# A gated cross-attention and mixture-of-experts kernel: setup in half chunks, in-place M for the first batch, transfers split, the last placing moved

## The chip, the cores and the metric

The kernel runs on one core of one Trainium2 chip. The core has five engines that run side by side, each with its own in-order instruction queue: TensorE (PE, matrix products and transposes, which write into PSUM), VectorE (DVE), ScalarE (ACT), GpSimd (POOL) and SyncE (SP). SP and POOL also issue the transfers (DMA) between memories. The metric is the device time of one execution in microseconds (us). Before the change the median of three runs is 1732.46 us (1730.8 to 1734.78).

## The reference

Four batches of 2048 tokens of width 512 pass through two blocks with residual connections. The first is cross-attention with 16 heads of width 64 to 77 context rows per batch; the second sends each token to the two best of ten experts, of which eight are true and two are null.

```python
def _L0_xattn_ref(x, context, ln_gamma, ln_beta, w_q, w_kv, w_out, b_out, gate):
...
    xn = _layernorm(x, ln_gamma, ln_beta)
    q = (xn @ w_q).reshape(B, SQ, NUM_HEADS, DIM_HEAD)
    kv = context @ w_kv
    k, v = jnp.split(kv, 2, axis=-1)
...
    scores = jnp.einsum('bqhd,bkhd->bhqk', q * SCALE, k)
    attn = jax.nn.softmax(scores, axis=-1)
    out = jnp.einsum('bhqk,bkhd->bqhd', attn, v).reshape(B, SQ, INNER)
    out = out @ w_out + b_out
    return out * jnp.tanh(gate[0])

def _L0_ffn_ref(inputs, gate_w, gate_b, expert_w, expert_b):
...
    gate_logits = x @ gate_w.T + gate_b
    gate_probs = jax.nn.softmax(gate_logits, axis=-1)
    weights, selected = jax.lax.top_k(gate_probs, TOP_K)
...
    expert_out = jnp.einsum('td,edh->teh', x, expert_w) + expert_b[None, :, :]
    out = jnp.einsum('te,teh->th', combine_w, expert_out)
    return out.reshape(inputs.shape[:-1] + (out.shape[-1],))
x = x + jnp.tanh(g_xattn[0]) * _L0_xattn_ref(_layernorm(x, axis=-1), ctx_1024, L0_xattn_ln_gamma, L0_xattn_ln_beta, L0_xattn_w_q, L0_xattn_w_kv, L0_xattn_w_out, L0_xattn_b_out, L0_xattn_gate)
x = x + jnp.tanh(g_ffn[0]) * _L0_ffn_ref(_layernorm(x, axis=-1), L0_ffn_gate_w, L0_ffn_gate_b, L0_ffn_expert_w, L0_ffn_expert_b)
```

## The kernel before

Everything is float32. The tokens are 64 tiles of 128. Because the context is short, the kernel folds the weights into it once per batch: M (`m_sb`, 512 x 1232) is w_q times the keys of all heads, so that the scores of a tile are one product with its normalized, transposed rows; VW (`vw`, 1232 x 512 and a row of bias) is the values times w_out, so that the attention output is one product of the transposed weights `aT` with it.

**Setup.** The context is transposed (`setup_context`), keys and values come out of w_kv (`setup_kv`), w_q is transposed (`setup_q`). `setup_m(c)` makes M for one chunk of 128 input columns, c = 0 to 3. For each of the 16 heads one product (64 rows, 308 columns: 77 context rows of four batches) lands in one of the three `mm` PSUM tiles, and `put` copies it into a stage, ScalarE (L535) and VectorE (L537) in turn. The stage is a borrowed SBUF buffer: that of `vw` for even chunks, of `gwb` for odd ones. Then SP moves batch 0's part of the stage into `m_sb` (L556) and those of the other three batches to DRAM (`m_all`, L558). After chunk 1, `step(-2)` prepares the first token tiles: a transpose, statistics, a normalization, a square root, a load.

`setup_vw(j)` makes VW for one pair of heads, j = 0 to 7: five products into `mm` tiles (`pv`, L565), copied into one of eight row buffers, and stored from there to DRAM (`vw_all`, L576), the even batches by SP and the odd ones by POOL. Scores and softmax of tiles 0 and 1 stand between the pairs, at j = 2 and j = 5; `attn_squares` follows at j = 4 and j = 7. `load_vw(0, ...)` brings batch 0's VW back from DRAM, blocks 0 to 6 after pair 6 and blocks 7 to 9 after pair 7.

**Token loop.** `step(i)` works on several tiles at once: scores of tile i + 1 (L281), the transpose of i + 2 (L261), `attend(i - 1)` (L353), gate logits of i - 2, and the rest on the other engines. `attn_squares` transposes 32 x 32 squares on VectorE (L336), and 16 moves by SP (L342) bring them to their places in `aT`. When a batch ends, `load_vw` brings the next batch's VW; it overwrites what `attend` has just read, and waits for it.

**Experts.** Normalized rows are scattered by expert into DRAM (`dispatch`, L466), from row buffers `rows`, nine of them. The last phase walks 118 slots of 128 rows: `slot_load` (SP, L834) brings a block into one of the buffers of `ring`, `slot_tr` transposes it (L863) and ScalarE copies it out (L866), `slot_pe` multiplies by the expert's weights (L889), `slot_out` adds the result up (L897, L898), and POOL gathers and scatters the sums (L847, L905). While the first slots run, `tail(q)` finishes the last token tile: its gate logits at q = 0 to 2, `choose` and `ratio` (L421, ScalarE) at q = 3, the placing (`weigh`, `place` L444, `dispatch` and the first table of blocks) at q = 5, the other tables at q = 7 and 8.

**Order.** The program runs under `manual_schedule`: each engine executes its instructions in the order in which the code issues them, and the framework adds the waits between engines.

Of the kernel before, what the change touches and what calls it, by code (L numbers as in the profile page):

```python
# [8 lines left out]
F32 = mybir.dt.float32  # L9
# [9 lines left out]
P = 128  # L19
# [5 lines left out]
def kernel(  # L25
# [88 lines left out]
    def mm_tile(name):  # L114
        return ps_m.tile([P, 512], F32, tag="mm", name=name)
# [215 lines left out]
    def attn_squares(i):  # L331


        a = attns[i % 2]
        n = -(-(COLS + 1) // 32) * 32
        nc.vector.transpose(a[:, :n], a[:, :n])  # L336
        v = a.rearrange("p (k j t) -> p k j t", j=4, t=32)
        aT = work.tile([P, NKC, P], F32, tag="aT", name=f"aT_{i}", bufs=2)
        for j in range(4):
            nk = len(range(j, n // 32, 4))  # L340
            for t in range(4):
                nc.sync.dma_start(  # L342
                    aT[j * 32 : (j + 1) * 32, :nk, t * 32 : (t + 1) * 32],
                    v[t * 32 : (t + 1) * 32, :nk, j, :],
                )
        aTs[i] = aT

    def attend(i):
        po = mm_tile(f"po{i}")
        aT = aTs.pop(i)  # L350
        for k in range(NKC):
            m = KLAST if k == NKC - 1 else P
            nc.tensor.matmul(  # L353
                po,
                aT[:m, k, :],
                vw[:m, k, :],
                start=(k == 0),
                stop=(k == NKC - 1),
            )
        pos_[i] = po  # L360

    def residual(i):
# [169 lines left out]
    def put(dst, src, dve=False):  # L532
# [3 lines left out]
        else:  # L536
            nc.vector.tensor_copy(dst, src)  # L537

    def setup_m(c):

        stage = (gwb_flat if c % 2 else vw_flat)[:, : B * COLS].rearrange("p (b n) -> p b n", b=B)
        for h in range(H):
            r = slice(h % 2 * DH, (h % 2 + 1) * DH)
            pm = mm_tile(f"pm{c}_{h}")
            nc.tensor.matmul(  # L545
                pm[:, :BK],
                wqT[r, h // 2, c * P : (c + 1) * P],
                kT[r, h // 2, :],
                start=True,
                stop=True,  # L550
            )
            put(
                stage[:, :, h * SK : (h + 1) * SK],
                pm[:, :BK].rearrange("p (b k) -> p b k", b=B),
            )
        nc.sync.dma_start(m_sb[:, c, :], stage[:, 0, :])  # L556
        for b in range(1, B):
            nc.sync.dma_start(m_all[b][:, c * COLS : (c + 1) * COLS], stage[:, b, :])  # L558

    def setup_vw(j, dve=False):  # L560

# [51 lines left out]
    def is_tile(i):  # L613
        return 0 <= i < NT

    def step(i):
# [15 lines left out]
            slot_tr(0)  # L632
            slot_tr(1)
        if is_tile(i - 1):
            attend(i - 1)
            if is_tile(i) and i % TPB == 0:
                load_vw(i // TPB)
        if is_tile(i - 2):
            choose(i - 2)
        if is_tile(i + 4):  # L640
# [27 lines left out]
            load_x(i + 5)  # L668
        if is_tile(i + 1):
            attn_squares(i + 1)  # L670
        e = i - (NT - TPB + 1)
        if 0 <= e < NE:
            nc.sync.dma_start(we[:, e], expert_w[e].rearrange("(c p) n -> p c n", p=P))
# [132 lines left out]
    ring = rows[1 : NRB - 3] + [  # L806
        attns[a][:, v * ROW : (v + 1) * ROW] for a in range(2) for v in range(2)
    ]
    ring += rows[NRB - 3 :] + [rows[0]]
    px_pool = []  # L810
    hss, toks, accs, hsTs, exps, pes, turn = {}, {}, {}, {}, {}, {}, [0, 0]

# [129 lines left out]
    def tail(q):  # L942

        i = NT - 1
        if q < 3:
            gate_logits(i, 3 * q, 3 * q + 3 if q < 2 else NG)
        elif q == 3:
            choose(i)
            ratio(i)
        elif q == 5:  # L950
            weigh(i // 2)
            place(i // 2)
            pc = count_rows(csum[0][:, 0])
            dispatch(i // 2)
            first_table(pc)
        elif q == 7:
            second_table()
        elif q == 8:
            part_table()

    with tc.manual_schedule():
# [14 lines left out]
            fill_pair(j)  # L976
        for c in range(NC):
            setup_q(c)
        for c in range(NC):
            setup_m(c)  # L980
            if c == 1:
                step(-2)
        for j in range(NPAIR):

            if j == 2 or j == 5:
                i = j // 3
                scores(i, 0)
                input_transpose(i + 1)
                scores(i, 1)
                softmax_exp(i, (0, 1))  # L990
                scores(i, 2)
                softmax_exp(i, (2,))
                ys[i + 2] = work.tile([P, D], F32, tag="y", name=f"y_{i + 2}", bufs=1)
                norm_apply(f"a{i + 2}", ys[i + 2], xs[i + 2])
                norm_stats(f"a{i + 3}", xs[i + 3])
                norm_root(f"a{i + 3}")
            if j == 4 or j == 7:
                softmax_div(j // 5)
                norm_shift(f"a{j // 5 + 3}")
                attn_squares(j // 5)  # L1000
            setup_vw(j, j in (2, 3, 5, 6))
            if j + len(vbd) < NPAIR:
                fill_pair(j + len(vbd))
            if j == 3:
                load_x(4)
                load_x(5)
                nc.sync.dma_start(vw[KLAST - 1 : KLAST, NKC - 1, :], b_out.unsqueeze(0))
            elif j == 6:
                load_vw(0, 0, 7)
        load_vw(0, 7)  # L1010
        nc.sync.dma_start(gwb, gate_w.partition_broadcast(P))
        for i in range(1, NT - 1):
            if i == SNAP + 3:
# [87 lines left out]
```

## Time and profile before

| | |
|---|---|
| median of three runs | 1732.46 us |
| the profiled execution | 1732.76 us |
| its span on the core | 1731.0 us |
| TensorE busy | 1685.1 us |
| VectorE, ScalarE, GpSimd busy | 1228.3, 934.6, 466.4 us |
| mean granted TensorE clock | 0.989 |
| first product of M, first of VW, start of the token loop | 49.68, 84.46, 171.46 us |

The profile is one execution, recorded by the hardware. "Busy" is the time in which an engine had an instruction running; for TensorE, whose products are pipelined, their ends are modelled, so that a busy TensorE can still be below its best rate. A row of the timeline begins with the start and the duration in us, then names the engine, the line of the kernel, the operation, the tile written and the tiles read, and how often; square brackets tell how long the engine had been idle and what ended it. "SPq" is SP issuing transfers. A row of waits gives the total, the number and the longest. In a row by stage, each engine has its busy time, followed by the granted TensorE clock as a share of full speed, the busy share of the transfer engines and GB/s.

### The profile page before, as it was taken

The page shows a single profiled execution, that of the slowest core. Times are in us where ns is not written, and L with a number is a line of the kernel's source. Part 1 is how long each engine was busy: PE and PEld are TensorE (multiplying, and loading weights), DVE is VectorE, ACT ScalarE, POOL GpSimd, SP SyncE. Part 2 cuts the span into 40 slices and gives each one's busy share as a digit, 9 for nine tenths or more (in the row PEclk, how much of TensorE's full clock was granted, in tenths as well). Part 3 has the DMA queues.
Part 4 walks back from the last instruction along what each step waited for, and adds up shares of the span by engine and source line. Part 5 has one row for each costly group of instructions (what it writes and reads, how often), then busy time and mean ns, then how long its engine had stood idle before and what let it go on. Part 6 is the DMA issues. An engine that isn't in the chain of part 4 may idle for free.

```text
span 1731.0 us, 22490 instructions
## 1 busy us (share of the span) xinstructions
PE 1685.1 (97%) x4938; PEld 851.0 (49%) x4938; DVE 1228.3 (71%) x3180; ACT 934.6 (54%) x3252; POOL 466.4 (27%) x617
## 2 busy tenths in 40 slices
PE   8897999999999999999999999999989999999997
PEld 6443545454445454545454545555434444444443
DVE  1443889898898989898989888989884333333333
ACT  2463777777776777677767776776421111111110
POOL 3031111121111111111112111211166556555564
PEclk9998999999999999999999999999989999999999
DMA  7477333346533435543335555554458665576752
GB/s 239 186 221 228 89 91 95 84 109 152 149 87 97 100 90 142 154 104 91 88 89 125 157 145 163 158 162 102 118 172 271 201 200 171 168 228 208 204 163 79
DMA packets 424540, 254.51 MB, mean 147 GB/s; under 512 B 349317, under 2 KB 353413, under 8 KB 424145
## 3 DMA queue, kind: packets, MB, share of 16 engines
q1 hardware_dynamic: 389873, 149.47, 35.0%
q0 software_dynamic: 34528, 103.55, 18.3%
q8 instruction: 44, 0.72, 0.2%
q14 instruction: 95, 0.78, 0.2%
HBM read 119.41 MB, written 100.52 MB: 127 GB/s over the span
## 4 chain that ended last, share of the span: by engine, by line
PE 93%; DMA 3%; DVE 2%; issue 1%; ACT 1%; SPq 0%; POOL 0%; POOLq 0%; DVEq 0%; ACTq 0%
PE po L353 31%; PE sc L281 30%; PE px L889 11%; PE pe L889 11%; PE str L863 3%; PE pkv L510 2%; PE pv L565 2%; PE xtr L261 2%; PE pm L545 1%; DMA vw<-vw_all 1%; DMA out_dram<-x 1%; DVE prod L373 0%; DMA vw<-in_ctx_dram 0%; SPq L342 0%; DMA acc<-out_dram,row 0%
## 5 line engine op out<-in xcount | busy, mean ns | idle before, releaser
L353 PE MATMUL po<-vw,aT 128*128 128x512 f32 (+1 forms) x1280 | 563.7, 595 | 10.7 <-DMA vw<-vw_all 5.5
L281 PE MATMUL sc<-m_sb,xnT 128*128 128x385 f32 (+1 forms) x1536 | 552.9, 510 | 0.0
L373 DVE CUSTOM_DVE_ANT_0 prod<-row,gwb,gbias 128x512 f32<-128x512 f32 x640 | 478.0, 747 | 17.9 <-ACT row L255 1.8
L353 PEld LDWEIGHTS po<-vw,aT 128*128 128x128 f32 (+1 forms) x1280 | 244.1, 191 | 314.3 <-issue 305.0
L281 PEld LDWEIGHTS sc<-m_sb,xnT 128*128 128x128 f32 x1536 | 284.0, 190 | 212.5 <-issue 86.3
L466 POOL DMA_INDIRECT hb<-row,dst x128 | 128.8, 1006 | 757.1 <-DVE nbh_h L250 677.8
L314 ACT ACTIVATE attn<-sc,nmx 128x77 f32<-128x77 f32 x1024 | 316.0, 347 | 28.4 <-DVE nmx L309 23.1
L866 ACT COPY m_sb<-str 128x512 f32<-128x512 f32 x118 | 68.5, 588 | 365.0 <-PE str L863 217.7
L314 ACT ACTIVATION_READ_ACCUMULATOR attn<-sc,nmx 128x1 f32 x1024 | 233.2, 228 | 0.0
L889 PE MATMUL px<-big,m_sb 128*128 (+1 forms) x472 | 214.7, 598 | 0.0
L889 PE MATMUL pe<-big,m_sb 128*128 (+1 forms) x472 | 212.3, 592 | 0.0
L897 DVE TENSOR_TENSOR yb<-px,blks 128x512 f32<-128x512 f32 x59 | 40.8, 692 | 130.1 <-PE px L889 97.4
L233 ACT ACTIVATE sdh_h<-mvh_h,eps_t 128x1 f32<-128x1 f32 x64 | 18.9, 295 | 205.9 <-DVE rsa_a L245 193.2
L889 PEld LDWEIGHTS px<-big,m_sb 128*128 128x128 f32 x472 | 86.2, 192 | 87.1 <-issue 87.0
L897 DVE TENSOR_TENSOR yb<-pe,blks 128x512 f32<-128x512 f32 x59 | 40.8, 692 | 123.3 <-PE pe L889 101.3
L889 PEld LDWEIGHTS pe<-big,m_sb 128*128 128x128 f32 x472 | 85.2, 190 | 85.6 <-issue 85.6
L303 DVE TENSOR_REDUCE mx<-sc 128x5 f32<-128x385 f32 (+1 forms) x192 | 106.2, 580 | 16.3 <-PE sc L281 14.1
L905 POOL DMA_INDIRECT out_dram<-acc,row x82 | 82.9, 1011 | 103.5 <-DVE acc L898 96.1
L364 DVE SCALAR_TENSOR_TENSOR x<-po,gx,x 128x512 f32<-128x512 f32 x64 | 48.0, 750 | 76.4 <-PE pp L444 45.1
L264 ACT ACTIVATE xnT<-xtr,bet,gam 128x128 f32<-128x128 f32 x256 | 95.4, 452 | 6.3 <-PE xtr L261 6.3
L327 DVE TENSOR_TENSOR attn<-attn,ri 128x1232 f32<-128x1232 f32 x64 | 92.3, 1442 | 5.1 <-DMA aT<-attn 0.8
L847 POOL DMA_INDIRECT acc<-out_dram,row x82 | 86.2, 1051 | 30.7 <-issue 29.8
(157 smaller groups left out, 1562.1 us busy)
## 6 DMA issues: line engine op xcount, KB each, us to landing
aT<-attn SPq DMA_DIRECT2D x768, 40.0 KB
row<-hb SPq DMA_DIRECT2D x71, 264.0 KB
x<-in_x_dram SPq DMA_DIRECT2D x64, 256.0 KB
out_dram<-x SPq DMA_DIRECT2D x64, 256.0 KB
aT<-attn SPq DMA_DIRECT2D x256, 36.0 KB
big<-in_L_ffn_expert_w_dram SPq DMA_DIRECT2D x8, 1024.0 KB
attn<-hb SPq DMA_DIRECT2D x31, 264.0 KB
vw<-vw_all SPq DMA_DIRECT2D x3, 2304.0 KB
```

The lines of the kernel that those rows point to most:

```text
L264: nc.scalar.activation(xnT[:, c, :], ptr[:, c, :], AF.Identity, bias=bet[:, c : c + 1], scale=gam[:, c : c + 1],)
L281: nc.tensor.matmul(t[:, : n1 - n0], xnTs[i][:, c, :], m_sb[:, c, n0:n1], start=(c == 0), stop=(c == NC - 1),)
L303: nc.vector.tensor_reduce(mx[:, g0:g1], scs[i, g][:, : (g1 - g0) * SK].rearrange("p (h k) -> p h k", k=SK), AX.X, ALU.max,)
L314: nc.scalar.activation(a[:, h * SK : (h + 1) * SK], t[:, k : k + SK], AF.Exp, bias=nm[:, h : h + 1], scale=SCALE, accum_out=sm[:, h : h + 1],)
L327: nc.vector.tensor_tensor(a, a, ri.unsqueeze(2).to_broadcast([P, H, SK]), ALU.mult)
L353: nc.tensor.matmul(po, aT[:m, k, :], vw[:m, k, :], start=(k == 0), stop=(k == NKC - 1),)
L373: nc.vector.tensor_tensor_reduce(prod, hrs[i][:, :D], gwb[:, e, :], 1.0, gbias[:, e : e + 1], ALU.mult, ALU.add, pgs[i][:, e : e + 1],)
L466: ins = nc.gpsimd.indirect_dma_start(out=hb[k], out_offset=bass.IndirectOffsetOnAxis(ap=dst[:, i % 2, k : k + 1], axis=0), in_=hr[:, :].bi ...
L847: ins = nc.gpsimd.indirect_dma_start(out=acc, out_offset=None, in_=of, in_offset=bass.IndirectOffsetOnAxis(ap=tok, axis=0), bounds_check=T ...
L889: nc.tensor.matmul(pe, hsT[:, c, :], w[:, c, :], start=(c == 0), stop=(c == NC - 1))
L897: nc.vector.tensor_tensor(tt, pe, b, ALU.add)
L905: ins = nc.gpsimd.indirect_dma_start(out=of, out_offset=bass.IndirectOffsetOnAxis(ap=tok, axis=0), in_=acc, in_offset=None, bounds_check=T ...
```

## The change

- **M of batch 0 in place, half chunks.** `setup_m` copies each head's product out of PSUM twice: the 231 columns of batches 1 to 3 into a stage, and batch 0's 77 columns straight into `m_sb`. The transfer into `m_sb` is gone. A stage holds eight heads instead of sixteen, and there are five: two in `vw`, two in `gwb`, one in the unused end of `big`. The other batches go to DRAM by halves.
- **Six PSUM tiles.** Odd heads use the `mm` tiles, even heads the three tiles of the scores.
- **`share`** replaces `put` here. It keeps a running cost for each of ScalarE and VectorE and gives a copy to the one with the lower sum: 3 for a wide copy, 2 for a narrow one.
- **`ahead`** takes the work of `step(-2)` apart into five pieces that run after given heads of chunks 1 and 2; each adds 9 to ScalarE's cost.
- **Moves of attn.** The 16 moves leave `attn_squares` and become `attn_move`. In setup those of tile 0 are issued by five, five and six before pairs 4, 5 and 6, and those of tile 1 after the last of `load_vw(0)`.
- **VW in three pieces at a switch.** `attend` calls back after the products of blocks 2, 5 and 9, and `load_vw` brings blocks 0 to 2, 3 to 5 and 6 to 9.
- **Late last placing.** In `tail`, the placing moves from q = 5 to 7, the tables from 7 and 8 to 9 and 10, and `ring` loses two of its thirteen buffers, those that hold the last two token tiles.

```diff
--- before.py
+++ after.py
@@ -336,16 +336,23 @@
         nc.vector.transpose(a[:, :n], a[:, :n])
         v = a.rearrange("p (k j t) -> p k j t", j=4, t=32)
         aT = work.tile([P, NKC, P], F32, tag="aT", name=f"aT_{i}", bufs=2)
-        for j in range(4):
-            nk = len(range(j, n // 32, 4))
-            for t in range(4):
-                nc.sync.dma_start(
-                    aT[j * 32 : (j + 1) * 32, :nk, t * 32 : (t + 1) * 32],
-                    v[t * 32 : (t + 1) * 32, :nk, j, :],
-                )
         aTs[i] = aT
-
-    def attend(i):
+        moves[i] = [
+            (
+                aT[j * 32 : (j + 1) * 32, : len(range(j, n // 32, 4)), t * 32 : (t + 1) * 32],
+                v[t * 32 : (t + 1) * 32, : len(range(j, n // 32, 4)), j, :],
+            )
+            for j in range(4)
+            for t in range(4)
+        ]
+
+    moves = {}
+
+    def attn_move(i, n0=0, n1=16):
+        for dst, src in moves[i][n0:n1]:
+            nc.sync.dma_start(dst, src)
+
+    def attend(i, after=None):
         po = mm_tile(f"po{i}")
         aT = aTs.pop(i)
         for k in range(NKC):
@@ -357,6 +364,8 @@
                 start=(k == 0),
                 stop=(k == NKC - 1),
             )
+            if after is not None and k in (2, 5, NKC - 1):
+                after(*{2: (0, 3), 5: (3, 6)}.get(k, (6, NKC)))
         pos_[i] = po
 
     def residual(i):
@@ -536,26 +545,74 @@
         else:
             nc.vector.tensor_copy(dst, src)
 
+    held = [0, 0]
+
+    def share(dst, src, cost):
+
+        n = int(held[1] < held[0])
+        held[n] += cost
+        if n:
+            nc.vector.tensor_copy(dst, src)
+        else:
+            nc.scalar.copy(dst, src)
+
+    between = {}
+
+    def ahead():
+
+
+        def apply():
+            ys[1] = work.tile([P, D], F32, tag="y", name="y_1", bufs=1)
+            norm_apply("a1", ys[1], xs[1])
+
+        def shift():
+            norm_shift("a2")
+            load_x(3)
+
+        between[1, 15] = lambda: input_transpose(0)
+        between[2, 3] = lambda: norm_stats("a2", xs[2])
+        between[2, 7] = apply
+        between[2, 11] = lambda: norm_root("a2")
+        between[2, 15] = shift
+
+    HALF = H // 2 * SK
+    room = (vw_flat, gwb_flat, vw_flat[:, 3 * HALF :], gwb_flat[:, 3 * HALF :], big[:, o:])
+    stages = [
+        r[:, : (B - 1) * HALF].rearrange("p (b n) -> p b n", b=B - 1) for r in room
+    ]
+
     def setup_m(c):
 
-        stage = (gwb_flat if c % 2 else vw_flat)[:, : B * COLS].rearrange("p (b n) -> p b n", b=B)
-        for h in range(H):
-            r = slice(h % 2 * DH, (h % 2 + 1) * DH)
-            pm = mm_tile(f"pm{c}_{h}")
-            nc.tensor.matmul(
-                pm[:, :BK],
-                wqT[r, h // 2, c * P : (c + 1) * P],
-                kT[r, h // 2, :],
-                start=True,
-                stop=True,
-            )
-            put(
-                stage[:, :, h * SK : (h + 1) * SK],
-                pm[:, :BK].rearrange("p (b k) -> p b k", b=B),
-            )
-        nc.sync.dma_start(m_sb[:, c, :], stage[:, 0, :])
-        for b in range(1, B):
-            nc.sync.dma_start(m_all[b][:, c * COLS : (c + 1) * COLS], stage[:, b, :])
+
+        for half in range(2):
+            stage = stages[(2 * c + half) % len(stages)]
+            for n in range(H // 2):
+                h = half * (H // 2) + n
+                r = slice(h % 2 * DH, (h % 2 + 1) * DH)
+                if h % 2:
+                    pm = mm_tile(f"pm{c}_{h}")
+                else:
+                    t = h // 2 % 3
+                    pm = ps_s.tile([P, 512], F32, tag=f"sc{t}", name=f"pm{c}_{h}")
+                nc.tensor.matmul(
+                    pm[:, :BK],
+                    wqT[r, h // 2, c * P : (c + 1) * P],
+                    kT[r, h // 2, :],
+                    start=True,
+                    stop=True,
+                )
+                share(
+                    stage[:, :, n * SK : (n + 1) * SK],
+                    pm[:, SK:BK].rearrange("p (b k) -> p b k", b=B - 1),
+                    3,
+                )
+                share(m_sb[:, c, h * SK : (h + 1) * SK], pm[:, :SK], 2)
+                if (c, h) in between:
+                    between[c, h]()
+                    held[0] += 9
+            for b in range(1, B):
+                a = c * COLS + half * HALF
+                nc.sync.dma_start(m_all[b][:, a : a + HALF], stage[:, b - 1, :])
 
     def setup_vw(j, dve=False):
 
@@ -632,9 +689,8 @@
             slot_tr(0)
             slot_tr(1)
         if is_tile(i - 1):
-            attend(i - 1)
-            if is_tile(i) and i % TPB == 0:
-                load_vw(i // TPB)
+            new = is_tile(i) and i % TPB == 0
+            attend(i - 1, (lambda k0, k1: load_vw(i // TPB, k0, k1)) if new else None)
         if is_tile(i - 2):
             choose(i - 2)
         if is_tile(i + 4):
@@ -668,6 +724,7 @@
             load_x(i + 5)
         if is_tile(i + 1):
             attn_squares(i + 1)
+            attn_move(i + 1)
         e = i - (NT - TPB + 1)
         if 0 <= e < NE:
             nc.sync.dma_start(we[:, e], expert_w[e].rearrange("(c p) n -> p c n", p=P))
@@ -806,7 +863,7 @@
     ring = rows[1 : NRB - 3] + [
         attns[a][:, v * ROW : (v + 1) * ROW] for a in range(2) for v in range(2)
     ]
-    ring += rows[NRB - 3 :] + [rows[0]]
+    ring += rows[NRB - 3 : NRB - 1]
     px_pool = []
     hss, toks, accs, hsTs, exps, pes, turn = {}, {}, {}, {}, {}, {}, [0, 0]
 
@@ -947,15 +1004,15 @@
         elif q == 3:
             choose(i)
             ratio(i)
-        elif q == 5:
+        elif q == 7:
             weigh(i // 2)
             place(i // 2)
             pc = count_rows(csum[0][:, 0])
             dispatch(i // 2)
             first_table(pc)
-        elif q == 7:
+        elif q == 9:
             second_table()
-        elif q == 8:
+        elif q == 10:
             part_table()
 
     with tc.manual_schedule():
@@ -976,10 +1033,9 @@
             fill_pair(j)
         for c in range(NC):
             setup_q(c)
+        ahead()
         for c in range(NC):
             setup_m(c)
-            if c == 1:
-                step(-2)
         for j in range(NPAIR):
 
             if j == 2 or j == 5:
@@ -998,6 +1054,8 @@
                 softmax_div(j // 5)
                 norm_shift(f"a{j // 5 + 3}")
                 attn_squares(j // 5)
+            if 4 <= j < 7:
+                attn_move(0, 5 * j - 20, 5 * j - 15 if j < 6 else 16)
             setup_vw(j, j in (2, 3, 5, 6))
             if j + len(vbd) < NPAIR:
                 fill_pair(j + len(vbd))
@@ -1008,6 +1066,7 @@
             elif j == 6:
                 load_vw(0, 0, 7)
         load_vw(0, 7)
+        attn_move(1)
         nc.sync.dma_start(gwb, gate_w.partition_broadcast(P))
         for i in range(1, NT - 1):
             if i == SNAP + 3:
```

## The prediction

> **What bounds the kernel now.** I read the engine table first, then what TensorE waited for, then the timeline of the stages that the diff touches.
>
> ```profile
> span 1731.0 us, 22490 instructions
> PE 1685.1 (97%) x4938; PEld 851.0 (49%) x4938; DVE 1228.3 (71%) x3180; ACT 934.6 (54%) x3252; POOL 466.4 (27%) x617
> ...
> PE pp L444 <- DVE msk L403: 8.3, 1, 8.3
> ...
> PE po L353 <- DMA vw<-vw_all: 5.5, 1, 5.5
> PE pm L545 <- ACT vw L535: 4.4, 1, 4.4
> PE pv L565 <- DVE row L537: 3.1, 1, 3.1
> PE po L353 <- DMA aT<-attn: 2.5, 1, 2.5
> PE po L353 <- issue: 1.5, 2, 1.0
> PE po L353 <- DMA out_dram<-x: 1.2, 1, 1.2
> ```
>
> TensorE is busy for 97% of the span, and the chain of waits is 93% TensorE. The token loop runs at 17.35 us a tile with no gap, and nothing in the diff alters its arithmetic. What the change can win lies in the lines above (all but pp and the last two are in the first 172 us), in what the clock loses after each of them, and in the M stage, where a busy TensorE is not at its peak:
>
> ```profile
> 55.79 0.94 ACT L535 COPY vw<-pm 128x308 f32<-128x308 f32 x2 [0.83 <-PE pm L545]
> 55.83 0.48 DVE L537 COPY vw<-pm 128x308 f32<-128x308 f32 x1 [0.39 <-PE pm L545]
> 56.26 0.82 PEld L545 LDWEIGHTS pm<-big 64*128 64x128 f32 x6 [0.47 <-ACT vw L535]
> ```
>
> Three heads' weights load in 0.82 us (0.27 us a head), and then the loads wait for a copy to free one of three PSUM tiles. A turn of six heads takes 2.65 us, 0.44 us a head. The stage runs from 49.68 to 84.46 (last copy ended 85.04): 35.4 us.
>
> **M stage, the one part that may lose.** Before, a head is one 308-column copy, 0.42 us on ACT or 0.48 on DVE, the engines alternating on different tiles. After, it is two: 231 columns into the stage, 77 into m_sb, from the same PSUM tile. Sizing them: a 512-column copy takes 0.59 (ACT) and 0.69 (DVE), so a column costs 0.83 and 1.03 ns and the rest is fixed, 0.16 on both. That gives 0.36 and 0.23 on ACT, 0.40 and 0.24 on DVE.
>
> How do the two stand to each other? `share` alternates: with costs 3 and 2 the sequence is ACT 231, DVE 77, DVE 231, ACT 77, then again. The two copies of a head always land on different engines. Taken by the rows alone, they overlap: (0.36+0.23+0.40+0.24)/4 = 0.31 us a head plus gaps, 20 to 22 us, and half of the 5.6 us of inserted ACT work: 26 us, a gain of 9.
>
> [...] No row here has two engines copying from one tile. But the trace does show order kept by tile: four transposes fill xtr from 145.09 to 145.69, and ACT, idle for 4.2 us and reading the first quarter first, starts at 145.73. [...] Together with the alternation that makes one chain over both engines: 0.36, hand-over, 0.24, 0.40, hand-over, 0.23, next pair. A hand-over between ACT and DVE costs 0.03 to 0.04 (sda ended 69.63, the reciprocal began 69.66; nmx ended 121.45, exp began 121.49); with 0.05 and a DVE gap of 0.04, two heads take 1.37 us, and 64 heads 44 us. After each inserted piece of ACT work the nine units of credit send about two heads wholly to DVE at 0.64, beside that work: 43 us. Bounds from the rows: 39 if ACT's back-to-back copies overlap by 0.1 (two 0.59 copies took 1.05), 58 if narrow copies cost what the nearest wide or narrow rows cost (ACT 0.42 and 0.35, the exp row of 77 columns; DVE 0.48 and 0.25; hand-overs and gap of 0.1: 1.80 for two heads). I take 43, since the two copy widths fix the slope. Six PSUM tiles don't help such a chain; they let TensorE start VW some 1.3 us before the last copy, and the sparse matmuls may cost 0.7 of clock. **M stage: 43 - 35.4 - 1.3 + 0.7 = +7 us** (+3 to +23).
>
> The stall of 4.4 in this stage (ACT doing statistics, apply and the square root in one piece at 64.35 to 69.6) is inside the 35.4, and goes: the same work is strewn over chunk 2 and DVE copies meanwhile. load_x(3) moves with it; it has 40 us until use. SP now issues 24 transfers instead of 16 (616 KB ones took 0.5 to 1.05 us to issue): at most 24 us under 43, hidden. Four SBUF transfers into m_sb (2.5 MB) vanish; scores(0) did not wait for them (it began at 93.14 as VW ended), so that is worth nothing. A stage is reused after five halves, 27 us later; four 616 KB transfers issued at 57.6 to 61.4 were gone by about 65. No wait.
>
> **VW and the first attend, the part that wins.**
>
> ```profile
> 116.62 11.99 SPq L342 DMA_DIRECT2D aT<-attn  x16
> 128.71 8.87 SPq L576 DMA_DIRECT2D vw_all<-row  x12
> 137.67 0.68 SPq L588 DMA_DIRECT2D vw<-vw_all  x1
> 141.46 18.08 SPq L342 DMA_DIRECT2D aT<-attn  x16
> 159.63 1.76 SPq L576 DMA_DIRECT2D vw_all<-row  x4
> 161.83 0.39 SPq L588 DMA_DIRECT2D vw<-vw_all  x1
> ...
> 165.00:170.00 5.00, 2.91 (x4) 1.36 (x5) 0.00 (x0) 0.00 (x0) 0.00 (x0) 0.50 1.03 389
> ```
>
> SP's queue is the cause. Sixteen aT moves stand before the row stores of pair 4, so the eight row buffers run out and pv waits 3.1 and 0.7. The second sixteen stand before the stores of pair 7, and the last three blocks of VW, which read those rows, are asked for at 161.83: po waits 2.5 and 5.5. The clock column drops to 0.50. Priced from the rows: VW start 84.46 to tile loop 171.46 is 87.0. Eighty pv at 0.434 (20 took 8.68) make 34.7, three blocks of scores at 8.72 make 26.2, one po is 8.6: 69.5. Of the 17.5 lost, 11.7 are the waits; the clock is the rest (16 pv in 8.9 instead of 6.9, 14 po in 7.7 for 6.0, 6 in 4.5 for 2.6).
>
> After, on the old clock without stalls: aT_0 in fives at 0.65 to 0.7 goes before pairs 4, 5, 6; pair 4's stores leave by 123, pair 5's by 129, pair 6's by 135.5, all in time for the row reuse at pairs 6 and 7. VW blocks 0 to 6 are asked for at 135.5, pair 7's stores leave at 137.5 to 139, blocks 7 to 9 by 140. From 135.5 about 3.7 MB (1.8 of VW, 1.26 of rows, 0.67 of VW) have to pass; at the 300 GB/s of 140 to 150 that is 12 us, to 148. attend(0) would start at 145.2. I leave 1.5 us of wait and 0.5 of clock: **-15.5 us** (-8 if the wait stays, -17.5 at best).
>
> What becomes late instead: aT_1, asked for after VW (140 to 154), needed by attend(1) at 164; then gwb at 155, landed by 163 (2.5 MB at 300 or more), while DVE wants it at about 160. Three us of DVE wait, ahead of the reductions of tile 3; scores of tile 4 need those PSUM tiles at 173. Hidden; without that cover, 1 to 3 us.
>
> **Switches.** At each of three switches VW is asked for when po is nearly over (431.24) and TensorE waits 1.18, 0.56 and 0.96, plus 0.2 of clock each: 3.3. The pieces let SP ask when it is free of aT, at 430.3, and po's first blocks no longer wait for the last. SP stands no longer at its wait than before. **-3 us** (0 to -3.3).
>
> **Late last placing.** The 8.3 us before pp looks like the prize. It isn't:
>
> ```profile
> 1283.83 0.29 ACT L421 ACTIVATE e<-v 128x1 f32<-128x1 f32 x1 [14.18 <-DVE v L401]
> 1284.03 1.05 ACT L866 COPY m_sb<-str 128x512 f32<-128x512 f32 x2
> ```
>
> ACT's `ratio` of the last tile stays at q = 3 and waits for the same DVE choice; the copies of slots 6 and 7 stand behind it. Without pp TensorE goes on to the transpose of slot 8, which needs slot 6's PSUM tile: copied at 1284.6, when it ran before too (1284.65). Gain 0. Dispatch slips from 1290 to about 1298.5, its rows land near 1306, and the first load from the late table leaves at about 1308; TensorE wants slot 16 at 1318. Eleven ring buffers instead of thirteen drop the two that waited for the scatter. **0** (0 to +3).
>
> **Sum:** +7 - 15.5 - 3 + 0 = -11.5. The span 1731.0 becomes 1719.5; with the 1.76 us around it, 1721.3. The profiled execution (1732.76) is 0.3 above the median shown, so **1721.0**.
>
> **Rivals.** (a) The two copies run side by side: M stage 26 us, -9.4 in place of +7: 1704.5. For it: the engines' rows alone. Against: order by tile in the trace. (b) Slower: the chain of narrow copies in the M stage. If they keep nearly the price of wide ones, 0.90 a head, the stage is 58 us: +23 - 18.5 = +4.5: 1737. It decides from 0.84 us a head (54 us), where it eats all gains. (c) VW's last blocks stay late, because the stores and 3.7 MB before attend(0) use the transfer engines that the aT moves gave up: -8 instead of -15.5: 1728.5.
>
> **Chances:** forecast 0.55 (its own range 1715 to 1727), (a) 0.12, (b) 0.20, (c) 0.13. The measurement tells 0.2% (3.5 us) from no change. Faster takes the forecast's 0.53, (a) and half of (c): 0.71; same the rest of these: 0.09; slower 0.20. The range goes from (a) to (b), 1704 to 1737.
>
> **What shows it.** M stage: copies of a head one after the other, ACT and DVE never both busy outside the inserted work, 0.65 to 0.70 us a head, TensorE leaving near 91. VW: no wait of pv for row; po's wait for vw under 3 us. Switches: no wait over 0.3. Tail: 8 us of TensorE idle still at slot 8, now put down to ACT. If the copies overlap or cost over 0.84 us a head, the sum is wrong.

## The result, and the profile after

| | before | after |
|---|---|---|
| median | 1733.1 us (1730.8 to 1734.78, 4 runs) | 1718.47 us (1717.48 to 1719.16, 4 runs) |
| span of the profiled execution | 1731.0 us | 1716.4 us |
| mean granted TensorE clock | 0.989 | 0.993 |

The changed kernel takes 0.9916 of the time, with a 95% interval from 0.9899 to 0.9933. The time is 2.5 us from the forecast of 1721.0, but two terms of the sum were wrong by 9 and 6.5 us in opposite directions and cancelled. The first products of each stage, read from the two timelines, say where the 14.6 us of span went:

| stretch | before | after | difference | forecast |
|---|---|---|---|---|
| first product of M to first of VW | 34.78 | 32.56 | -2.2 | +7 |
| first of VW to the first scores of the token loop | 87.00 | 77.96 | -9.0 | -15.5 |
| from there to `attend` of the tile before the first switch | 251.86 | 253.84 | +2.0 | 0 |
| lead at that point, to lead at `attend` of the last tile (three switches) | 9.24 | 12.65 | -3.4 | -3 |
| lead there, to lead when slot 9's product begins (tail) | 12.65 | 14.77 | -2.1 | 0 |

(In the last two rows "before" and "after" are how far the changed kernel is ahead at the two ends of the stretch.) First the engine table and what TensorE waited for, of the changed kernel:

```profile
span 1716.4 us, 22604 instructions
PE 1679.2 (98%) x4938; PEld 849.3 (49%) x4938; DVE 1231.6 (72%) x3222; ACT 934.1 (54%) x3274; POOL 464.8 (27%) x617
...
PE str L920 <- ACT m_sb L923: 8.8, 3, 7.8
PE po L360 <- DVE ri L326: 3.9, 1, 3.9
PE pm L597 <- DVE m_sb L555: 3.1, 7, 0.8
PE pp L453 <- DVE msk L412: 1.1, 1, 1.1
PE pv L622 <- ACT row L544: 1.1, 1, 1.1
PE xtr L261 <- ACT y L255: 0.5, 1, 0.5
```

The waits of `po` at the switches are gone, the waits for the aT moves too; `pv` waits 1.1 us instead of 3.8 (3.1 and 0.7); `po` still waits 3.9 us once, and the stall of the tail has changed its name and little of its length.

**M stage.** The timeline of the copies shows what the forecast called a chain over both engines:

```profile
52.02 0.24 DVE L555 COPY m_sb<-pm 128x77 f32<-128x77 f32 x1 [0.54 <-ACT vw L557]
52.17 0.39 DVE L555 COPY vw<-pm 128x231 f32<-128x231 f32 x1
52.59 0.22 ACT L557 COPY m_sb<-pm 128x77 f32<-128x77 f32 x1 [0.61 <-DVE vw L555]
52.71 0.36 ACT L557 COPY vw<-pm 128x231 f32<-128x231 f32 x1
53.10 0.24 DVE L555 COPY m_sb<-pm 128x77 f32<-128x77 f32 x1 [0.55 <-ACT vw L557]
```

The second copy of a head waits for the first, on the other engine, with a hand-over of 0.03 to 0.04 us, and each engine is idle for 0.54 to 0.61 us in every turn. From 52.02 to 53.10, two heads take 1.08 us, not 1.37. The rows have the durations that were forecast (0.36 and 0.22 on ACT, 0.39 and 0.24 on DVE); but two copies that follow each other on one engine don't stand end to end. DVE's wide copy starts 0.15 us after the narrow one of 0.24 began, ACT's 0.12 after the one of 0.22. The last copy ends at 84.36, 34.6 us after the first product of M (49.72), where the stage before had 35.4. This stage varies little: in the six other profiles with the same code for it, the first product of VW comes 32.54 to 32.59 us after the first of M.

**VW and the first `attend`.** SP's queue:

```profile
113.92 5.14 SPq L353 DMA_DIRECT2D aT<-attn  x5
119.16 1.86 SPq L633 DMA_DIRECT2D vw_all<-row  x4
121.35 3.57 SPq L353 DMA_DIRECT2D aT<-attn  x5
125.02 2.06 SPq L633 DMA_DIRECT2D vw_all<-row  x4
127.13 6.77 SPq L353 DMA_DIRECT2D aT<-attn  x6
134.00 2.37 SPq L633 DMA_DIRECT2D vw_all<-row  x4
136.46 0.39 SPq L645 DMA_DIRECT2D vw<-vw_all  x1
136.94 4.60 SPq L633 DMA_DIRECT2D vw_all<-row  x4
149.34 0.39 SPq L645 DMA_DIRECT2D vw<-vw_all  x1
```

From the table of waits, SP's wait for stores into `vw_all` to land; from the timeline, a copy of ScalarE that waits for a row buffer, and the first `attend`:

```profile
SPq L645 <- DMA vw_all<-row: 7.7, 1, 7.7
```

```profile
133.50 0.59 ACT L544 COPY row<-pv 128x512 f32<-128x512 f32 x1 [4.90 <-DMA vw_all<-row]
...
148.94 11.46 PE L360 MATMUL po<-vw,aT 128*128 128x512 f32 x20 [3.90 <-DVE ri L326]
```

The moves stand between the row stores as planned, but the row buffers still run out: ScalarE waits 4.90 us for one, and 1.1 us of that reaches TensorE. The stores of pair 7 (136.94 to 141.5) stand behind the load of blocks 0 to 6 (136.46), and the last blocks, which read what those stores write, are asked for only at 149.34: SP waits 7.7 us for the stores to land. TensorE's wait of 3.90 us is put down to DVE's `ri`. That row is tile 2's (it ended at 148.25), while `attend` works on tile 0; experiment 4 shows that TensorE doesn't need it and that the wait is one for the loads. The product then runs slower, 11.46 us against 8.75 in the loop: the granted clock is 0.77 from 148.94 to 160.30, and 1.00 from 168.96 to 177.60.

One profile of this stretch is not exact. Four of the experiments below (5 to 8) leave the code as it is up to the last load of VW, and their profiles have 75.22 to 77.64 us for it, against the 77.96 here. So the gain of the stretch is 9.0 to 11.8 us, and differences of less than 3 us between two profiles of it say nothing of an edit.

**The gate weights.** The first use of `gwb` by VectorE:

```profile
170.78 0.75 DVE L382 CUSTOM_DVE_ANT_0 prod<-row,gwb,gbias 128x512 f32<-128x512 f32 x1 [6.54 <-DMA gwb<-in_L_ffn_gate_w_dram]
```

**Tail.** The timeline at slot 8:

```profile
1270.29 0.30 ACT L430 ACTIVATE e<-v 128x1 f32<-128x1 f32 x1 [13.29 <-DVE v L410]
1270.49 1.05 ACT L923 COPY m_sb<-str 128x512 f32<-128x512 f32 x2
1271.11 1.12 PE L920 MATMUL str<-ident,attn 128*128 128x128 f32 x4 [7.76 <-ACT m_sb L923]
1272.02 4.50 PE L946 MATMUL px<-big,m_sb 128*128 x8
```

TensorE is idle for 7.76 us (8.33 before) and the wait is now ACT's, as forecast: `ratio` waits for VectorE, and the copies of two slots stand behind it.

### The profile page after: what moved, and what is told of

It reads as the page before. It is cut to its first block, busy times and chain, and to the rows that moved or that the text cites. A ratio compares the mean times of both kernels' runs of the same rounds, so it can differ in the third digit from the quotient of the medians.

```text
span 1716.4 us, 22604 instructions
## 1 busy us (share of the span) xinstructions
PE 1679.2 (98%) x4938; PEld 849.3 (49%) x4938; DVE 1231.6 (72%) x3222; ACT 934.1 (54%) x3274; POOL 464.8 (27%) x617
## 5 line engine op out<-in xcount | busy, mean ns | idle before, releaser
L303 DVE TENSOR_REDUCE mx<-sc 128x5 f32<-128x385 f32 (+1 forms) x192 | 106.2, 580 | 20.2 <-PE sc L281 18.1
L962 POOL DMA_INDIRECT out_dram<-acc,row x75 | 76.2, 1017 | 93.6 <-DVE acc L955 85.9
L336 DVE STREAM_TRANSPOSE attn<-attn 128x1248 f32<-128x1248 f32 x64 | 94.1, 1471 | 0.0
```

The lines of the kernel that those rows point to most:

```text
L303: nc.vector.tensor_reduce(mx[:, g0:g1], scs[i, g][:, : (g1 - g0) * SK].rearrange("p (h k) -> p h k", k=SK), AX.X, ALU.max,)
L962: ins = nc.gpsimd.indirect_dma_start(out=of, out_offset=bass.IndirectOffsetOnAxis(ap=tok, axis=0), in_=acc, in_offset=None, bounds_check=T ...
```

## The experiments

All edits are against the changed kernel. The theory to begin with: the M stage gains little because one tile's two copies make one chain over two engines; VW and the first `attend` gain because the moves no longer stand before the stores, and lose part of it to the late last blocks and to the late `gwb`; the tail's stall belongs to `ratio`. The rivals stand in each expectation. The experiments were measured on several chips, so the ratios to the kernel before are the surer comparison; two kernels less than some 0.2% apart are not told apart.

**1. Both copies of a head on one engine.**

```diff
-    def share(dst, src, cost):
+    def share(pairs, cost):
         n = int(held[1] < held[0])
         held[n] += cost
-        if n:
+        for dst, src in pairs:
...
-                share(stage[...], pm[:, SK:BK]..., 3)
-                share(m_sb[:, c, h * SK : (h + 1) * SK], pm[:, :SK], 2)
+                share(((stage[...], pm[:, SK:BK]...),
+                       (m_sb[:, c, h * SK : (h + 1) * SK], pm[:, :SK])), 5)
```

> The changed kernel, but both copies of a head go to one engine (chosen by the running cost, 5 a head), so that no copy waits for another engine. Theory (the M stage is one chain through both engines because the two copies of a PSUM tile are ordered): the chain falls apart into two, about 0.55 us a head on VectorE and 0.48 on ScalarE, or 0.27 a head in all, where the loads of the weights become the limit; first product of M to first product of VW falls from 32.6 us to about 20, and the time by 9 to 12 us, to 1707 to 1710. Rival (the copies are bound by their own fixed prices, or the stores of M and their stages set the pace): the stage stays above 28 us and the time within 4 us of 1718.5.

Measured: 1705.14 us (1703.59 to 1706.17), ratio 0.9843 (0.9826 to 0.9859). From M's first product (49.93) to VW's (70.15) it is 20.2 us instead of 32.6. The same copies, of the same sizes, from the same tiles:

```profile
51.78 0.36 ACT L558 COPY vw<-pm 128x231 f32<-128x231 f32 x1
51.83 0.40 DVE L556 COPY vw<-pm 128x231 f32<-128x231 f32 x1
52.03 0.23 ACT L558 COPY m_sb<-pm 128x77 f32<-128x77 f32 x1
52.14 0.23 DVE L556 COPY m_sb<-pm 128x77 f32<-128x77 f32 x1
52.30 0.35 ACT L558 COPY vw<-pm 128x231 f32<-128x231 f32 x1
```

Now the engines work side by side, each on a tile of its own: two heads in 0.52 us (51.78 to 52.30) instead of 1.08. What follows: the chain over two engines cost the change 12 us, all of it by the choice of engine for the second copy.

**2. Three PSUM tiles instead of six in the M stage.**

```diff
-                if h % 2:
-                    pm = mm_tile(f"pm{c}_{h}")
-                else:
-                    t = h // 2 % 3
-                    pm = ps_s.tile([P, 512], F32, tag=f"sc{t}", name=f"pm{c}_{h}")
+                pm = mm_tile(f"pm{c}_{h}")
```

> The changed kernel with the three mm tiles alone for M, as before the change. Theory (the M stage is one chain through two engines, so PSUM tiles don't pace it): from the first product of M to the last copy nothing changes by more than 1 us, VW's first product starts at most 2 us later, and the time stays within 2 us of 1718.5. Rival (the six tiles are what made the stage shorter): a head takes as long as a third of a turn of product and two copies, over 0.6 us, and the time rises by more than 4 us.

Measured: 1720.65 us (1718.95 to 1721.92), ratio 0.9934 (0.9916 to 0.9953).

```profile
51.99 0.24 DVE L555 COPY m_sb<-pm 128x77 f32<-128x77 f32 x1 [0.55 <-ACT vw L557]
52.15 0.39 DVE L555 COPY vw<-pm 128x231 f32<-128x231 f32 x1
...
53.08 0.24 DVE L555 COPY m_sb<-pm 128x77 f32<-128x77 f32 x1 [0.55 <-ACT vw L557]
```

The pace is 1.09 us for two heads, as with six: the tiles don't pace the chain. VW's first product comes at 85.04 instead of 82.28. Six tiles are worth that head start of TensorE over the copies, 2 to 3 us. (What `ahead` is worth, the other part of the change in this stage, no run tells apart.)

**3. All sixteen moves of a tile at once, as before.**

```diff
                 attn_squares(j // 5)
-            if 4 <= j < 7:
-                attn_move(0, 5 * j - 20, 5 * j - 15 if j < 6 else 16)
+                attn_move(j // 5)
...
         load_vw(0, 7)
-        attn_move(1)
```

> The changed kernel with the moves of attn in setup put back as before: all 16 at once, before the stores of pair 4 and of pair 7. Theory (their place in SP's queue is what the VW stage gained from): pv waits about 3 us for row buffers again, blocks 7 to 9 of VW are asked for near 159, and the time rises by 8 to 10 us, to about 1727. Rival (the stage is faster because of the missing transfers into m_sb and the smaller backlog of M stores, not because of the moves): less than 4 us of loss.

Measured: 1727.27 us (1726.12 to 1728.29), ratio 0.9974 (0.9963 to 0.9985). The waits of TensorE:

```profile
PE po L360 <- DMA vw<-vw_all: 6.9, 1, 6.9
...
PE pv L622 <- DVE row L546: 3.6, 1, 3.6
```

The 8.8 us that are lost (0.6% by the ratios) are those of the stage: the token loop begins at 170.89 instead of 160.24. (The later loop finds `gwb` in time, asked for at 161.78, and 2 us come back.) From VW's first product it is 88.59 us, where the kernel before has 87.00: the new places of the moves carry all that the stretch gained. The run undoes both at once. By the waits, `pv` pays for tile 0's moves, which stand in one block before the stores again, and `po` for tile 1's: the last blocks are asked for at 160.79.

**4. VW of batch 0 in small pieces, each after its pair.**

```diff
-            elif j == 6:
-                load_vw(0, 0, 7)
-        load_vw(0, 7)
+            if j >= 2:
+                load_vw(0, (j - 1) * 2 * SK // P if j > 2 else 0, j * 2 * SK // P)
+        load_vw(0, 8)
```

> The changed kernel, but batch 0's VW is brought back in small loads after pairs 2 to 7 (blocks 0 and 1 after pair 2, then 2, 3, 4 and 5, 6, 7), and only blocks 8 and 9 after the last stores. Theory (attend(0) waits because 1.8 MB of VW stand in the queue ahead of pair 7's stores, so that blocks 7 to 9 are asked for only at 149): SP asks for the last blocks by about 143, the wait of po falls from 3.9 to under 1 us, po of tile 0 takes 9 instead of 11.5 us, the time falls by 4 to 7 us. Rival (the transfer engines are full in this stretch, so loading earlier only delays the row stores): pv waits for row buffers by as much as po gains, the time stays within 2 us of 1718.5.

Measured: 1718.69 us (1717.46 to 1721.63), ratio 0.9928 (0.9912 to 0.9945): no gain. Yet the stage gained. SP's queue, the first `attend` and `ri` of tile 2; then SP's wait for the last stores, and VectorE's first use of `gwb`:

```profile
140.96 2.85 SPq L633 DMA_DIRECT2D vw_all<-row  x4
...
145.61 0.34 SPq L645 DMA_DIRECT2D vw<-vw_all  x1
...
147.74 8.75 PE L360 MATMUL po<-vw,aT 128*128 128x512 f32 x20
...
150.86 0.25 DVE L326 RECIPROCAL ri<-sm 128x16 f32<-128x16 f32 x1 [2.08 <-ACT attn L314]
```

```profile
SPq L645 <- DMA vw_all<-row: 1.3, 1, 1.3
```

```profile
169.50 0.75 DVE L382 CUSTOM_DVE_ANT_0 prod<-row,gwb,gbias 128x512 f32<-128x512 f32 x1 [9.16 <-DMA gwb<-in_L_ffn_gate_w_dram]
```

With no 1.8 MB load ahead of pair 7's stores, SP waits 1.3 us for them instead of 7.7, the blocks that read them are asked for 3.7 us earlier (145.61), `po` waits for nothing and takes 8.75 us. It starts 3 us before `ri` runs, so the wait put down to `ri` was one for the loads. The token loop begins at 156.33, 3.9 us before the changed kernel's and 0.7 to 3.9 us before those of experiments 5 to 8. But `pv` waits 3.4 us in four places, and `gwb` is asked for only 1.2 us earlier (159.68, as the moves before it took 12.36 us instead of 10.51) and lands at 169.5. So VectorE waits 9.16 us instead of 6.54, TensorE waits 2.7 us for the rows behind it, and at the first switch 0.9 us of the 3.9 are left.

**5. `gwb` before the moves of tile 1.**

```diff
         load_vw(0, 7)
-        attn_move(1)
         nc.sync.dma_start(gwb, gate_w.partition_broadcast(P))
+        attn_move(1)
```

> The changed kernel, but the gate weights (gwb, 2.5 MB) are loaded before the moves of attn of tile 1 instead of after them. Theory (VectorE's wait of 6.5 us for gwb at 164 to 171 costs the 2 us that the kernel loses between the start of the token loop and the first switch): that wait falls below 2 us, the waits of xtr for y (0.5) and of pp for msk (1.1) vanish, the loop's first ten tiles are 2 us shorter, the time falls by about 2 us. Rival (the moves of tile 1 then come late, behind 2.5 MB): attend(1) waits for aT, and the time stays or rises by up to 5 us.

Measured: 1714.76 us (1714.26 to 1716.42), ratio 0.9907 (0.9889 to 0.9925). VectorE's row at 161.97 has no wait, `xtr` and `pp` wait for nothing, and from the start of the loop to `attend` before the first switch it is 252.48 us instead of 253.84, near the 251.86 of before. So the late `gwb` cost some 1.4 of the 2.0 us. The rest of this run's lead is a shorter wait for VW (2.72 us), which the edit doesn't touch. By the ratios the whole gain is 0.09%, inside what they tell apart.

**6. VW in one piece at a switch, as before.**

```diff
-            attend(i - 1, (lambda k0, k1: load_vw(i // TPB, k0, k1)) if new else None)
+            attend(i - 1)
+            if new:
+                load_vw(i // TPB)
```

> The changed kernel with VW loaded in one piece after attend at a batch's end, as before. Theory: po waits at the three switches for 0.6 to 1.2 us each again and the clock takes 0.2 us more each time, together 3.4 us, to about 1722. Rival (the loop is so far ahead or behind in its transfers that the waits don't come back): within 1 us of 1718.5.

Measured: 1720.51 us (1719.97 to 1721.71), ratio 0.9939 (0.9921 to 0.9957). The waits at the switches are back:

```profile
PE po L360 <- issue: 4.1, 3, 2.2
...
PE po L360 <- DMA out_dram<-x: 1.1, 1, 1.1
```

(The longest "issue", 2.2, is that of setup.) The waits are 1.1 and 1.9 us, and from `attend` before the first switch to that of the last tile it is 831.56 us instead of 827.89 (831.30 before the change), with 2 us by the medians and 4 by the ratios: the pieces are worth about the 3 us of the forecast.

**7. The placing at q = 5, as before.**

```diff
-    ring += rows[NRB - 3 : NRB - 1]
+    ring += rows[NRB - 3 :] + [rows[0]]
...
-        elif q == 7:
+        elif q == 5:
...
-        elif q == 9:
+        elif q == 7:
...
-        elif q == 10:
+        elif q == 8:
```

> The changed kernel with the last placing at q = 5, the tables at 7 and 8, and the ring of thirteen buffers, as before. Theory (ScalarE's ratio holds TensorE there in both, so that moving the placing is worth nothing but a different phase of the clock): TensorE's idle time before the next transpose is 7.5 to 8.5 us in both, and the time stays within 2 us of 1718.5. Rival (the 2.1 us that the changed kernel gained between attend of the last tile and slot 9 belong to the move): the time rises by 2 us or more.

Measured: 1717.11 us (1716.68 to 1719.13), ratio 0.9916 (0.9899 to 0.9934), the ratio of the changed kernel itself.

```profile
1272.33 0.19 PE L453 MATMUL pp<-msk,upper 128*128 128x40 bf16 x1 [7.97 <-DVE msk L412]
...
1273.55 5.25 PE L946 MATMUL px<-big,m_sb 128*128 x8
```

Moving the placing is worth nothing. The 2.1 us of the stage table are in part the products after the stall: eight of them took 5.85 us in the profile of before, 5.25 here, 4.50 in the changed kernel and 5.73 in the kernel of experiment 9, against 3.60 in the slots that follow. The granted clock over them was 0.60 before (1285.56 to 1291.24) and 0.79 in the changed kernel (1272.02 to 1276.35), and 1.00 in the slots that follow in both. The time of these products varies with no edit that touches it.

**8. `ratio` at q = 6.**

```diff
         elif q == 3:
             choose(i)
+        elif q == 6:
             ratio(i)
```

> The changed kernel, but ScalarE's ratio of the last tile is issued at q = 6 instead of q = 3, behind the copies of slots 6 to 8. Theory (in the tail ScalarE's ratio, not the placing, holds TensorE): the 7.8 us of TensorE idle time before slot 8 shrink below 2, the clock doesn't fall after it, the time falls by 6 to 10 us. Rival (VectorE is the limit there, or slot 16's block comes late because the late table is ready no sooner): TensorE stops a few slots later instead, and the time falls by less than 3 us.

Measured: 1716.22 us (1713.33 to 1720.97), ratio 0.9912 (0.9891 to 0.9934). The stall of 7.8 us at slot 8 is gone, and two others come:

```profile
1275.30 0.17 PE L774 MATMUL pc<-cs,ones_b 128*128 128x20 bf16 x1 [2.61 <-DVE acc L955]
...
1275.93 5.39 PE L946 MATMUL px<-big,m_sb 128*128 x8
...
1302.18 0.66 PE L920 MATMUL str<-ident,attn 128*128 128x128 f32 x4 [1.49 <-ACT m_sb L923]
```

From `attend` of the last tile to slot 9 it is 38.13 us instead of 42.68; 1.5 us are given back at slot 16. The stall was ACT's queue. The 3 us that are left hardly show in the run's time: in its profile the token loop began 1.2 us before the changed kernel's, but `xtr` waited 2.7 us for ScalarE's `y`, as it did in experiment 4 behind the late `gwb`, so that `attend` of the last tile came 1.5 us later, and the ratio is the changed kernel's within what can be told apart.

**9 to 11. Together.** Three kernels, measured side by side on one chip: experiments 1 and 5 together; the same with 8; the same with 8 and 4.

> Both copies of a head on one engine (M stage 20.4 instead of 32.6 us) and the load of gwb ahead of the moves of tile 1. If the gains of the two edits lie in different stages they add up: 1718.5 - 13.3 - 3 = 1702, between 1700 and 1704; M stage 20 us, no wait of VectorE for gwb over 1 us, no wait of xtr for y. The rival: with the M stage shorter everything in setup asks for its transfers earlier while they take as long, so that the wait for VW or for tile 1's moves grows by what gwb gave: 1705, as with the one-engine copies alone.

> The same with the square root of the last tile's choice (ratio) at q = 6 instead of q = 3. If the 7.8 us stall at slot 8 is ScalarE's queue behind ratio, and what is given back (2.6 us at pc, 1.5 at slot 16) is all, it is 2 to 3 us faster than the kernel of the same call without it: 1699 to 1700. The rival, that the stall only moves, gives no difference within 1 us.

> The same as the one with ratio at q = 6, and VW of batch 0 loaded in six small pieces after pairs 2 to 7. With gwb early, the 4 us that the early pieces won at the start of the token loop, and that were lost again to the wait for gwb when they were tried alone, should stay: 1695 to 1697, po's first wait 0, a loop start 3 to 5 us earlier than in the two others. The rival: the pieces stand in SP's queue before the row stores, so pv waits 3 us for row buffers, and the late gwb and tile 1's moves take the rest: no faster than without them, within 1.5 us.

| kernel | median us | ratio |
|---|---|---|
| 1 + 5 | 1704.25 (1703.9 to 1706.71) | 0.9836 (0.9823 to 0.985) |
| 1 + 5 + 8 | 1699.21 (1696.85 to 1701.09) | 0.9803 (0.9789 to 0.9817) |
| 1 + 5 + 8 + 4 | 1699.58 (1695.26 to 1701.81) | 0.9812 (0.9798 to 0.9827) |

1 and 5 together are no faster than 1 alone. No wait of VectorE for `gwb` is left, but tile 1's moves, issued right behind that load, took 17.1 us instead of 10.5, and the second `attend` waited 1.3 us for them: the rival's mechanism. Still, from the start of the loop to `attend` before the first switch it is 253.39 us, against 254.69 in 1 alone. What hides this gain of 1.3 us in the profile is the VW stretch before it, longer by 2.0 us (`pv` waited 4.3 us instead of 1.0), where the edit of 5 changes nothing. Late `ratio` takes off 5 us more by the medians, twice the expectation: the tail to slot 9 takes 36.93 us instead of 44.21, and slot 16 gives 1.77 back. The TensorE rows of the tail in that kernel:

```profile
1258.97 0.18 PE L453 MATMUL pp<-msk,upper 128*128 128x40 bf16 x1 [0.39 <-DVE i L411]
1259.00 0.18 PE L453 MATMUL pp<-cs,ones_b 128*128 128x40 bf16 x1
1261.78 0.17 PE L779 MATMUL pc<-cs,ones_b 128*128 128x20 bf16 x1 [2.61 <-DVE yb L959]
1261.88 0.63 PE L925 MATMUL str<-ident,row 128*128 128x128 f32 x4
1262.42 3.70 PE L951 MATMUL px<-big,m_sb 128*128 x8
```

The products after the shorter wait take 3.70 us, where the kernel without the edit needed 5.73: 2 us of the difference lie in these eight products. They are no sure part of the gain. In experiment 8 they took 5.39 us after a wait of the same 2.61 us, where the kernel without that edit needed 4.50. The small pieces of VW bring the loop forward by 5 to 6 us (143.60 against 149.61 and 148.96), but the profiled execution is the fastest of its five (1695.26 us), and that of 1 + 5 + 8 the slowest of its own (1701.09). The medians of the last two kernels are the same: by them, early pieces are worth nothing that can be measured. `pv` waits 4.2 us for rows in it, which the rival named. Whether a part of the gain is real is left open. The version to keep is 1 + 5 + 8: 1699.21 us, 0.9803 of the time before, where the change alone had 0.9916.

## Why the prediction was right, and where it was not

That the total came within 2.5 us is luck in part: the M stage was priced 9.2 us too dear, the VW stretch 6.5 us too cheap in this profile. Each term on its own says more.

**M stage: the right mechanism, a wrong size, and with it the wrong sign.** That the second copy of a head waits for the first was the author's assumption, preferred to the engines' bare rows, and the changed kernel's timeline bears it out: from 50.54 to 67.92, where the two copies of a head run on different engines, the second begins 0.03 to 0.04 us after the first has ended. No run has such a pair side by side on two engines. The step that failed is the term "with 0.05 and a DVE gap of 0.04, two heads take 1.37 us". The hand-over measured 0.03 to 0.04, there is no gap, and a narrow copy hides 0.09 to 0.10 us of itself under the wide one that follows on its engine: twice in two heads, 0.2 us, with hand-overs and gap the other 0.1. The row that would have told it was quoted, two 0.59 copies in 1.05, but was used only for the lower bound, 39 us, and only for ACT. The stage was taken as 43 us to the last copy and measured 34.6, below that bound. TensorE's start before the last copy, taken as 1.3, is 2.1. The 0.7 us of clock was the author's guess, and no run shows it as a term: VW's first 20 products took 9.27 us in the changed kernel and 8.85 before, with 1.00 of the clock granted in both. The sum also mixes two ends: the 35.4 of before runs to the last copy, 0.6 us after VW's first product, so that its terms give +7.6 and not +7. Measured from M's first product to VW's, it is 34.64 - 2.08 - 34.78 = -2.2.

**Rival (b), dear narrow copies,** fell with that: narrow copies of 0.22 to 0.24 us. **Rival (a), 1704.5,** fell for this kernel and names what it left out: with each head on one engine the stage takes 20 us and the kernel 1705.1. (That the two times are so near is chance; the rival had 26 us for the stage and the full 15.5 for the VW stretch.)

**VW and the first `attend`: -9.0 instead of -15.5.** The step that failed is "pair 7's stores leave at 137.5 to 139, blocks 7 to 9 by 140", and with it the 1.5 us of wait. Leaving is not landing: the blocks wait until the stores have arrived, and these were asked for after 1.8 MB on the same queue. 3.9 us of wait, 2.9 of slow product and 1.1 of `pv` make up 7.9 of the 8.5 us above the stall-free 69.5. The 12 us were meant for all 3.7 MB, with the last blocks among them; TensorE began 12.5 us after the first load was issued (136.46 to 148.94), and only then were the last blocks asked for. Nor did the row stores leave "all in time for the row reuse": the 1.1 us of `pv` are a wait for a row. So rival (c) came true in its stage, at nearly its price of -8 in this profile and some 3 us better in the best of the four others, and its total of 1728.5 missed mainly because the M stage gained what it was thought to lose.

**`gwb`: "Hidden" was wrong.** VectorE could start with it at 170.78, not 163: the moves before it began at 150.29, not 140, so that it was asked for at 160.90, not 155, and it took 9.9 us, not 8. VectorE waited 6.5 us, and the stretch lost 2.0, of which experiment 5 gives some 1.4 back: inside the 1 to 3 that the forecast named without the cover.

**Switches: -3.4 for -3.** Right, and shown by taking the pieces away.

**Late last placing: 0.** Right in mechanism: 7.76 us of idle at slot 8, put down to ACT, and no difference when it is moved back. The 2.1 us in the stage table are mostly the products after the stall (5.85 us before, 4.50 after); no cause was shown for the wait that is shorter by 0.6 us.

## What to carry to other kernels

When one PSUM tile is read by two copies, put both on the same engine and let the other engine take the next tile: alternating them made one chain out of two engines here, at twice the time (1.08 us for two heads against 0.52). When transfers are moved up in a queue, price the arrival of what depends on them and not the issue (here the stores were issued by 141.5 and let their reader go at 149.34), and list what else stands in the queue behind; three of the gains here went, in part or whole, to the next load in line. The work moved off the stall was worth nothing here, while another engine's queue waited for the same result (TensorE idle for 7.76 us with the placing late, 7.97 with it at its old place): find that queue's head first.

## What the runs showed of the hardware

- Two PSUM copies in a row on one engine overlap in the records: in the changed kernel a 77-column copy of 0.22 to 0.24 us lets the next start 0.12 to 0.15 us after its own start (52.02 to 52.71), and in experiment 1 a wide copy and a narrow one together take 0.52 us (51.78 to 52.30) where their rows sum to 0.58 (ACT) and 0.63 (DVE). In these series a row's duration was not the pitch.
- In the changed kernel, four row stores issued between 136.94 and 141.5, behind a load of 1.8 MB on the same queue, let their reader go only at 149.34, 7.7 us after SP began to wait for them; in experiment 4, with no such load ahead, four stores issued from 140.96 to 143.8 let theirs go at 145.61, after 1.3 us.
- After an idle 8 us, eight products took 4.50 to 5.85 us instead of 3.60, differently in kernels whose code at that place is the same (4.50 in the changed kernel, 5.73 in that of experiment 9); the granted clock over them was 0.79 at 4.50 and 0.60 at 5.85. After 2.6 us of idle they took 3.70 us in one profile and 5.39 in another. A difference of 1 us behind such a stall, in one profile each, says nothing of an edit.
